# A four-layer graph network in fp32: two more dense layers in seven block products, norm sums moved to ScalarE, adjacency blocks kept by DMA

## The chip, the cores and the metric

The kernel runs on one core of a Trainium2 chip. The metric is the device time of one execution in microseconds (us). Before the change the median of three runs is 2434.67 us (2434.01 to 2434.8). TensorE is called PE here (PEld is its weight load), VectorE DVE, ScalarE ACT, GpSimd POOL, and SyncE, which issues most DMAs, SP.

## The reference

There are B = 32 graphs of N = 512 nodes with D = 256 features, and a dense 512 x 512 adjacency for each. Everything is fp32. Each of four layers ends in `x = layernorm(x + layer(x))`:

```
layer 0: h = (1 + eps) x + adj x;  relu(h W1 + b1) W2 + b2            hidden width 512
layer 1: h = adj (x W^T + b);      where(h > 0, h, alpha h)
layer 2: h = layer_norm(x) gamma + beta
         x + relu((adj h) Wrel + b_rel + h Wroot)
layer 3: h = (eps x + adj x) W1 + b1;  silu(rmsnorm(h) w) W2 + b2     hidden width 1024
```

The terms with eps are put on the diagonal of the adjacency ("loops"), so layer 0 multiplies by adj + (1 + eps) I, layers 1 and 2 by adj, layer 3 by adj + eps I.

## The kernel before

**Plan.** The kernel body describes every operation to a planner (`Plan`, L182). An operation may have several ways (engines) with a cost each (L35 to L68). `order` (L304) plays the list forward, gives each operation an engine, a place in that engine's queue and a buffer, and `best` (L298) keeps the rule from `RULES` (L83) whose plan ends first. The instructions are then issued in that fixed order, so each engine works through its queue strictly in order. A rule says by how much the graphs are set apart (period), how fast need grows within a graph (pace), how far apart the last graphs are (last), and how early side work is wanted (near). Up to FLIGHT = 4 graphs are in flight. Buffers come from 38 rooms of 4 KB per partition, 12 small ones and 8 PSUM banks (L437 to L439); the numbers behind a pool say how many must be left for older graphs. All instructions carry line L252, since one helper issues them, so groups are told apart by tile names.

**Seven products.** `seven` (L552) multiplies two 2 x 2 block matrices with seven block products in place of eight (m1 to m7), at the price of sums of blocks: `left_sums` (L570) and `weight_sums` (L586) for the one factor, `right_sums` (L578) for the other. It is used for the aggregation adj x (`aggregate`, L653), for the first dense layer of layers 0 and 3 (`dense_feat`, L693), and for the second dense layer of layer 3, written out in `layer3` (L895 to L935). The sums of blocks may run on DVE or on POOL.

**Plain dense layers.** The second dense layer of layer 0 (L817 to L819), that of layer 1, and the two of layer 2 (L860 to L865) are done by `dense_tok` (L681): for each half of the nodes, 2 chunks by 4 factors, 16 products with 256 columns per layer and graph in layers 0 and 2, which are added to the residual on DVE by one 512-wide add per half.

**Norms.** `Norm.half` (L755) takes mean and variance of each 128-node chunk by DVE's batch-norm pair (stats and aggregate). `scales` (L761) makes 1/sqrt(var + eps) with a power on POOL, and `scaled` (L769) applies it, per chunk on ACT or DVE.

**Loops.** `Adjacency.sums` (L615) forms the block sums of an adjacency and copies the diagonal blocks aside (on POOL or ACT), `with_loops` (L636) writes them back with the loop added (POOL or DVE), `restore` (L632) writes them back plain (POOL or ACT).

**Queues.** SP's queue holds, in planned order, the loads of adjacencies (4 of 256 KB per graph), of x and of weights, and the stores of the results.

Of the kernel before, what the change touches and what calls it, by code (L numbers as in the profile page):

```python
# [53 lines left out]

def gpsimd_time(n):
    return 0.15 + n * 0.0024, 0.05
# [10 lines left out]
def spread_time():  # L67
# [15 lines left out]
RULES = [  # L83
    (period, pace, 12, near)
    for period, pace in ((60, 1), (76, 1), (84, 2))
    for near in (0, 1, 2, 4)
]
# [94 lines left out]
class Plan:  # L182
# [53 lines left out]
    def do(self, out, *ways, ordered=None):  # L236

        ins = []
        port = set()
        for e, method, _, args, kw in ways:  # L240
            tiles = [x for x in (*args, *kw.values()) if isinstance(x, (bass.AP, Part))]
            ins += tiles
            if e == "gpsimd" and kw.get("op") != ALU.pow or e == "vector" and not (
                method.startswith("bn_") or any(in_psum(x) for x in tiles)
            ):
                port.add(e)

        def issue(engine, method, args, kw):
            def put(x):
                return x.place() if isinstance(x, Part) else x  # L250

            getattr(getattr(self.nc, engine), method)(  # L252
                put(out), *(put(x) for x in args), **{k: put(x) for k, x in kw.items()}
            )

        self.add(
            {
                e: (times, lambda e=e, m=method, args=args, kw=kw: issue(e, m, args, kw))
                for e, method, times, args, kw in ways
            },  # L260
            out, ins, ordered, port,
        )

    def move(self, engine, out, src, times, inward=True):


        def issue():
            getattr(self.nc, engine).dma_start(  # L268
                *(x.place() if isinstance(x, Part) else x for x in (out, src))
            )  # L270

        self.add({engine: (times, issue)}, out if inward else None, [] if inward else [src])
# [114 lines left out]
def tile_gnn_stack(ctx: ExitStack, tc: tile.TileContext, a: dict, out: bass.AP):  # L387
# [36 lines left out]
    FLIGHT, ROOMS, SMALL = 4, 38, 12  # L424
# [12 lines left out]
    banks = pool(psum, "ps", 8, N, N, (0, 2, 2))  # L437
# [23 lines left out]

    def copy(o, x):
        plan.do(o, scalar(AF.Copy, span(o), x), vector("tensor_copy", span(o), x))
# [17 lines left out]
    def stt(o, x, s, y, op0, op1):  # L481
        plan.do(o, vector("scalar_tensor_tensor", span(o), x, s, y, op0=op0, op1=op1))

# [64 lines left out]
    mhalf = constant("mhalf", [P, 2 * NC])  # L548
    nc.vector.memset(mhalf, -0.5)
# [20 lines left out]
    def left_sums(left, a21, s):  # L570

        sub(s[2], left["m1"], a21, vector, gpsimd)
        add(s[0], a21, left["m4"], vector, gpsimd)
        sub(s[1], s[0], left["m1"], vector, gpsimd)
        sub(s[3], left["m2"], s[1], vector, gpsimd)
        left.update(m5=s[0], m6=s[1], m7=s[2], m3=s[3])

    def right_sums(b11, b12, b21, b22, t):  # L578

        sub(t[0], b12, b11)  # L580
        sub(t[1], b22, t[0])
        sub(t[2], b22, b12, vector, gpsimd)
        sub(t[3], b21, t[1], vector, gpsimd)
        return dict(m1=b11, m2=b21, m3=b22, m4=t[3], m5=t[0], m6=t[1], m7=t[2])
# [8 lines left out]
    def quarters(W):  # L593

        n = W.shape[-1] // 2
        return (W[:, k, i * n : (i + 1) * n] for i in range(2) for k in range(2))


    class Adjacency:
# [15 lines left out]
        def sums(self):  # L615
# [6 lines left out]
                with_diagonal.strided(0, (N + P, HC), (TH, 2), (1, P)),  # L622
            ]
            kept = room(4 * HC, P)
            self.plain = [
                kept[:, 0:HC], kept[:, HC : 2 * HC],
                kept[:, 2 * HC :].then(lambda v: v.rearrange("p (k s) n -> p k s n", s=2)),
            ]
            for d, o in zip(self.plain, self.loops):
                plan.do(d, gpsimd("tensor_copy", span(o), o), scalar(AF.Copy, span(o), o))  # L630

        def restore(self):  # L632
            for d, o in zip(self.plain, self.loops):
                plan.do(o, gpsimd("tensor_copy", span(o), d), scalar(AF.Copy, span(o), d))

        def with_loops(self, loop):  # L636
            for d, o in zip(self.plain, self.loops):
                wide = loop.unsqueeze(1)
                if len(o.shape) == 4:
                    wide = wide.unsqueeze(1)  # L640
                add(o, d, wide.to_broadcast(list(o.shape)), gpsimd, vector)

        def row_sums(self):
# [3 lines left out]
            add(rows[:, TH:N], s1[:, 0, :], s1[:, 1, :], gpsimd, vector)  # L647
            add(rows[:, 0:TH], a11[:, 0, :], a11[:, 1, :], gpsimd, vector)
            for k in range(HC):
                add(rows[:, 0:TH], rows[:, 0:TH], a12[:, k, :], gpsimd, vector)  # L650
            return rows

    def aggregate(x, adjacency):  # L653
# [6 lines left out]
        right = right_sums(*blocks, [t[:, i] for i in range(4)])  # L660
# [32 lines left out]
    def dense_feat(aT, left, bias, hT, done):  # L693
# [3 lines left out]
        t = room(4, TH)  # L697
        right = right_sums(
            *(aT[:, k, j * TH : (j + 1) * TH] for k in range(2) for j in range(2)),
            [t[:, i, :] for i in range(4)],  # L700
        )
# [24 lines left out]

    def column_sums(t, put):
# [16 lines left out]
    class Norm:  # L744


        def __init__(self, r):
            self.r = r
            few = small(64)
            cut = lambda at, n: few[:, at : at + n]  # L750
            self.st = [cut(6 * c, 6) for c in range(NC)]
            self.mv = cut(24, 2 * NC).then(lambda v: v.rearrange("p (c i) -> p c i", i=2))
            self.ve, self.rstd, self.shift = (cut(32 + 8 * i, 8) for i in range(3))

        def half(self, h):  # L755
            for c in range(h * HC, (h + 1) * HC):
                r = self.r[:, c, :]
                plan.do(self.st[c], ("vector", "bn_stats", stats_time(D), (r,), {}))
                plan.do(self.mv[:, c, :], ("vector", "bn_aggr", stats_time(6), (self.st[c],), {}))

        def scales(self, *affine):  # L761

            n = self.n = len(affine) * NC
            for i, (m, plus) in enumerate(affine):
                o = self.ve[:, i * NC : (i + 1) * NC]
                ts(o, self.mv[:, :, 1], m, plus, ALU.mult, ALU.add)
            inv_sqrt(self.rstd[:, 0:n], self.ve[:, 0:n])

        def scaled(self, i=0):  # L769
# [3 lines left out]
            stt(shift, self.mv[:, :, 0], -1.0, s, ALU.mult, ALU.mult)  # L773
            for c in range(NC):
# [4 lines left out]
                        "tensor_scalar", D, r, self.mv[:, c, 0:1], scale,  # L779
                        op0=ALU.subtract, op1=ALU.mult,  # L780
# [27 lines left out]
    def layer0(x, adjacency):  # L808
# [8 lines left out]
        for h in range(2):  # L817
            ps = dense_tok([(h1.chunk(k), W2_0[:, k, :]) for k in range(FC0)], h)
            add(half(x, h), ps, half(x, h))  # L819
            norm.half(h)  # L820
# [29 lines left out]
    def layer2(h, xx, u, adjacency):  # L850
# [9 lines left out]
        for h in range(2):  # L860
            ps = dense_tok(
                [(hT.chunk(k), Wroot[:, k, :]) for k in range(DC)]
                + [(aT[:, k, :], Wrel[:, k, :]) for k in range(DC)], h,
            )
            add(half(u, h), ps, half(u, h))  # L865
            stt(half(xx, h), half(u, h), 0.0, half(xx, h), ALU.max, ALU.add)
            norm.half(h)
        adjacency.with_loops(loop3)
# [3 lines left out]
    def layer3(x, adjacency, b):  # L872
# [5 lines left out]
        def squares(f):  # L878
            sq = room(2, N)
            act(sq, hT.pair(f), AF.Square)  # L880
            if f == 0:
                add(acc, sq[:, 0, :], sq[:, 1, :], vector, gpsimd)
            else:
                add(acc, acc, sq[:, 0, :], vector, gpsimd)
                add(acc, acc, sq[:, 1, :], vector, gpsimd)
# [9 lines left out]
        t1, t2, t4 = (room(FH, TH) for _ in range(3))  # L895
        for q in range(0, FH, 2):
# [3 lines left out]
            b11, b12 = (hT.pair(q)[:, :, j * TH : (j + 1) * TH] for j in range(2))  # L900
            b22 = hT.pair(FH + q)[:, :, TH:N]
            t1q, t2q = t1[:, q : q + 2], t2[:, q : q + 2]
            sub(t1q, b12, b11)
            sub(t2q, b22, t1q)
            sub(b12, b22, b12, vector, gpsimd)
            sub(t4[:, q : q + 2], hT.pair(FH + q)[:, :, 0:TH], t2q, vector, gpsimd)
        norm = Norm(x)

        def block(i, j):
            return x[:, j * HC : (j + 1) * HC, i * P : (i + 1) * P]  # L910

        def factor(m, k):
            if m in ("m4", "m5", "m6"):
                return dict(m4=t4, m5=t1, m6=t2)[m][:, k, :]
            f = k if m in ("m1", "m7") else FH + k
            j = 0 if m in ("m1", "m2") else 1
            return hT.chunk(f)[:, j * TH : (j + 1) * TH]

        def product(m, ps, first):
            for k in range(FH):  # L920
                for i in range(HC):
                    mm(
                        ps[:, i, :], factor(m, k)[:, i * P : (i + 1) * P], A2_3[m][:, k, :],
                        first and i == 0 and k == 0, k == FH - 1,
                    )

        def take(ps, i, j):
            add(block(i, j), ps, block(i, j))

        def put(ps, i, j, more):  # L930
            take(ps, i, j)
            if i == 1:
                norm.half(j)

        seven(*(bank(HC, P) for _ in range(3)), product, take, put)  # L935
# [17 lines left out]
    W2_0 = weight("L0_gnn_W2")  # L953
    alpha = row("L1_gnn_alpha")
# [12 lines left out]
    add(shift_2, shift_2, b_2)  # L967
    h = layer1(x, adjacency)
# [9 lines left out]
    A2_3 = weight_sums(  # L978
        "A2_3",
        *(W2_3[:, k * FH : (k + 1) * FH, i * P : (i + 1) * P] for i in range(2) for k in range(2)),  # L980
    )
# [47 lines left out]
```

## Time and profile before

| | |
|---|---|
| profiled execution | 2439.81 us, span of the records 2438.0 us |
| median of the three runs | 2434.67 us |
| granted TensorE clock | 0.997 on average |
| PE, PEld busy | 98%, 87% of the span |
| DVE busy | 2050.2 us, 84% |
| ACT busy | 1226.0 us, 50% |
| POOL busy | 622.6 us, 26% |
| q1, the queue of the DMAs from SP | 71.05 MB, 8.7% of 16 DMA engines |

The busy time of an engine is the union of its instructions' times. Instructions of one engine overlap at their ends, so the mean time of one is longer than the step from one start to the next. An fp32 product appears in the profile as two MATMUL records and two LDWEIGHTS records: 1536 records of one group are 768 products, or 24 per graph.

### The profile page before, as it was taken

Reading aid. Unit: us, or ns where it says so; the run is one execution under the profiler, and the core shown is the slowest. Engines: PE = TensorE matmul, PEld = TensorE weight load, DVE = VectorE, ACT = ScalarE, POOL = GpSimd, SP = SyncE. Lnnn points to the kernel's source line nnn. Section 1 sums busy time; section 2 is a strip of 40 time slices with the busy share of each in tenths; the row PEclk is TensorE's granted clock in tenths of the full one; section 3 lists DMA queues with packets and bytes.
Section 4 is the critical chain, followed back from the end, with each engine's and each line's share of the span. In section 5 each row is a group of like instructions: output and inputs, shape, how many; then the busy total and the mean of one; then the engine's idle time right before and its main releaser. Section 6 shows DMA issues by size and latency. Waiting matters only on the chain.

```text
span 2438.0 us, 35804 instructions
## 1 busy us (share of the span) xinstructions
PE 2387.9 (98%) x12808; PEld 2117.5 (87%) x12808; DVE 2050.2 (84%) x5249; ACT 1226.0 (50%) x2490; POOL 622.6 (26%) x677
## 2 busy tenths in 40 slices
PE   7999999999999999999999999999999999999998
PEld 6888888888888888888888888888888888888888
DVE  7888888788888889888898788988888888888788
ACT  3454545545455454554554544545445455454464
POOL 2232222222222212232122232223222222222220
PEclk9999999999999999999999999999999999999999
DMA  5011001110011110111101111011110011101000
GB/s 177 1 35 35 10 26 35 36 35 10 27 35 35 35 35 1 35 35 35 35 1 35 35 35 36 1 35 35 35 35 9 28 35 36 35 1 35 1 1 35
DMA packets 34915, 73.89 MB, mean 30 GB/s; under 512 B 6832, under 2 KB 9648, under 8 KB 34736
## 3 DMA queue, kind: packets, MB, share of 16 engines
q1 hardware_dynamic: 30576, 71.05, 8.7%
q8 instruction: 101, 1.65, 0.3%
q10 hardware_dynamic: 4160, 0.54, 0.1%
q14 instruction: 78, 0.64, 0.1%
HBM read 54.80 MB, written 16.78 MB: 29 GB/s over the span
## 4 chain that ended last, share of the span: by engine, by line
PE 71%; DVE 23%; ACT 2%; DMA 2%; issue 1%; SPq 0%; POOL 0%; POOLq 0%; ACTq 0%; DVEq 0%
PE ps L252 71%; DVE room L252 19%; DVE few L252 4%; ACT room L252 2%; DMA room<-in_adj_dram 1%; DMA L_gnn_b<-in_L_gnn_b_dram 0%; SPq L268 0%; DMA room<-in_x_dram 0%; POOL few L252 0%; POOL room L252 0%; ACT L252 0%; POOLq L1025 0%; DVEq L252 0%; ACTq L1025 0%; ACTq L252 0%
## 5 line engine op out<-in xcount | busy, mean ns | idle before, releaser
L252 PE MATMUL ps<-room,room 128*128 128x256 f32 x3584 | 872.5, 382 | 20.7 <-DMA room<-in_x_dram 9.9
L252 PEld LDWEIGHTS ps<-room,room 128*128 128x128 f32 x3584 | 672.5, 191 | 122.3 <-DVE room L252 14.5
L252 DVE TENSOR_TENSOR room<-ps,room 128x256 f32<-128x256 f32 (+1 forms) x1024 | 523.7, 522 | 232.8 <-PE ps L252 194.6
L252 PE MATMUL ps<-L_gnn_W,room 128*128 128x128 f32 (+1 forms) x3584 | 623.0, 322 | 5.3 <-ACT room L252 3.4
L252 ACT ACTIVATE room<-room 128x1024 f32<-128x1024 f32 (+2 forms) x421 | 324.3, 773 | 564.2 <-DVE room L252 293.9
L252 PEld LDWEIGHTS ps<-L_gnn_W,room 128*128 128x128 f32 x3584 | 538.4, 191 | 58.1 <-ACT room L252 8.6
L252 DVE TENSOR_TENSOR room<-room,room 128x512 f32<-128x512 f32 (+1 forms) x825 | 491.4, 603 | 17.1 <-DMA room<-in_adj_dram 7.4
L252 POOL TENSOR_TENSOR few<-few,mhalf 128x4 f32<-128x4 f32 (+1 forms) x160 | 191.1, 1195 | 861.1 <-DVE few L252 860.7
L252 PE MATMUL ps<-room,L_gnn_W 128*128 128x256 f32 x1536 | 395.8, 380 | 2.2 <-DVE room L252 2.1
L252 ACT ACTIVATE room<-ps,L_gnn_b_c 128x256 f32<-128x256 f32 x768 | 314.5, 469 | 154.3 <-PE ps L252 149.8
L252 ACT ACTIVATE room<-ps 128x256 f32<-128x256 f32 (+1 forms) x510 | 200.5, 404 | 334.0 <-PE ps L252 327.9
L252 ACT ACTIVATE room<-room,few 128x256 f32<-128x256 f32 x531 | 282.9, 590 | 80.3 <-DVE few L252 79.6
L252 PEld LDWEIGHTS ps<-room,L_gnn_W 128*128 128x128 f32 x1536 | 286.8, 190 | 41.5 <-DVE room L252 4.8
L252 DVE TENSOR_TENSOR room<-room 128x256 f32<-128x256 f32 (+1 forms) x490 | 240.6, 505 | 82.3 <-DMA room<-in_adj_dram 62.3
L252 PE MATMUL ps<-room,A 128*128 128x256 f32 x1152 | 286.1, 380 | 1.1 <-DVE room L252 0.7
L252 POOL TENSOR_TENSOR room<-room,L_gnn_b 128x256 f32<-128x256 f32 x256 | 191.7, 764 | 324.4 <-PE ps L252 164.4
L252 PEld LDWEIGHTS ps<-room,A 128*128 128x128 f32 x1152 | 213.8, 190 | 30.1 <-ACT room L252 1.8
L252 POOL TENSOR_TENSOR room<-room,room 128x512 f32<-128x512 f32 (+1 forms) x103 | 117.0, 1137 | 380.5 <-ACT room L252 165.8
L252 PE MATMUL ps<-A,room 128*128 128x128 f32 x1536 | 195.8, 277 | 11.3 <-DVE room L252 11.1
L252 ACT ACTIVATE room<-room,L_gnn_rms_weight_c 128x512 f32<-128x512 f32 x256 | 168.8, 714 | 68.5 <-DVE room L252 68.1
L252 PEld LDWEIGHTS ps<-A,room 128*128 128x128 f32 x1536 | 184.3, 192 | 21.0 <-DVE room L252 16.3
L252 DVE BATCH_NORM_STATS2 few<-room 128x6 f32<-128x256 f32 x512 | 198.2, 403 | 0.4
(49 smaller groups left out, 1537.4 us busy)
## 6 DMA issues: line engine op xcount, KB each, us to landing
room<-in_adj_dram SPq DMA_DIRECT2D x128, 256.0 KB, 4.8
room<-in_x_dram SPq DMA_DIRECT2D x32, 512.0 KB, 5.8
out_dram<-room SPq DMA_DIRECT2D x32, 512.0 KB, 3.0
L_gnn_W<-in_L_gnn_W_dram SPq DMA_DIRECT2D x2, 1024.0 KB, 8.2
L_gnn_W<-in_L_gnn_W_dram SPq DMA_DIRECT2D x2, 512.0 KB, 6.8
L_gnn_b<-in_L_gnn_b_dram ACTq DMA_DIRECT2D x3, 128.0 KB, 4.2
L_gnn_W_rel<-in_L_gnn_W_rel_dram SPq DMA_DIRECT2D x1, 256.0 KB, 5.6
L_gnn_W_root<-in_L_gnn_W_root_dram SPq DMA_DIRECT2D x1, 256.0 KB, 5.3
```

Source lines behind the costliest of these rows:

```text
L252: getattr(getattr(self.nc, engine), method)(put(out), *(put(x) for x in args), **{k: put(x) for k, x in kw.items()})
```

## The change

1. The second dense layer of layer 0, and both dense layers of layer 2 as one, are done in seven products (`dense_add`, fed by `dense_sums`), as layer 3's was; layer 3 now calls the same two functions. For it the weights `A2_0` and `A_2` are summed once at the start.
2. `Norm.half` no longer uses DVE's batch-norm pair. ACT sums each chunk (`Identity` with an accumulator output), DVE turns the sums of two chunks into minus the mean, ACT sums the squares of x minus mean (`Square` with that bias), and `scales` and `scaled` work from these.
3. The diagonal blocks are kept and put back by DMAs within SBUF, issued from SP: four copies and four restores of 128 KB per graph, in place of three and three operations on POOL or ACT.
4. The sums of blocks, of rows and the loop adds are on DVE alone; POOL keeps the bias rows (`plus_row`) and the powers. `right_sums` puts one of its results in place, so that a room less is needed.
5. The planner gets other rules (period 50, pace 2, last 12 or 20, near 2), 36 rooms in place of 38, and keeps one PSUM bank instead of two for older graphs. The order before was made by period 84, pace 2, last 12, near 2; the one after by period 50, pace 2, last 20, near 2.

```diff
-RULES = [
-    (period, pace, 12, near)
-    for period, pace in ((60, 1), (76, 1), (84, 2))
-    for near in (0, 1, 2, 4)
-]
+RULES = [(50, 2, last, 2) for last in (12, 20)]
...
-    FLIGHT, ROOMS, SMALL = 4, 38, 12
+    FLIGHT, ROOMS, SMALL = 4, 36, 12
...
-    banks = pool(psum, "ps", 8, N, N, (0, 2, 2))
+    banks = pool(psum, "ps", 8, N, N, (0, 1, 1))
...
+    def total(o, x, func, **kw):
+        way = "scalar", "activation", total_time(span(x)), (x,), dict(func=func, **kw)
+        plan.do(o, way, scrap=scrap[:, 0 : span(x)])
...
+    def carry(o, x):
+        plan.move("sync", o, x, move_time(P * span(o) / 256))
...
-        sub(s[2], left["m1"], a21, vector, gpsimd)
+        sub(s[2], left["m1"], a21)
...
             for d, o in zip(self.plain, self.loops):
-                plan.do(d, gpsimd("tensor_copy", span(o), o), scalar(AF.Copy, span(o), o))
+                carry(d, o)
...
+    def dense_sums(upper, lower):
+        right = {}
+        for pairs in zip(upper, lower):
+            blocks = [x[:, :, j * TH : (j + 1) * TH] for x in pairs for j in range(2)]
+            sums = right_sums(*blocks, [room(2, TH) for _ in range(3)], blocks[1])
+            for m, x in sums.items():
+                right.setdefault(m, []).extend(x[:, e, :] for e in range(2))
+        return right
+
+    def dense_add(x, right, left, done):
+        def block(i, j):
+            return x[:, j * HC : (j + 1) * HC, i * P : (i + 1) * P]
+        def product(m, ps, first):
+            n = len(right[m])
+            for k in range(n):
+                for i in range(HC):
+                    mm(
+                        ps[:, i, :], right[m][k][:, i * P : (i + 1) * P], left[m][:, k, :],
+                        first and i == 0 and k == 0, k == n - 1,
+                    )
+        def take(ps, i, j):
+            add(block(i, j), ps, block(i, j))
+        def put(ps, i, j, more):
+            take(ps, i, j)
+            if i == 1:
+                done(j)
+        seven(*(bank(HC, P) for _ in range(3)), product, take, put)
...
         def half(self, h):
-            for c in range(h * HC, (h + 1) * HC):
-                r = self.r[:, c, :]
-                plan.do(self.st[c], ("vector", "bn_stats", stats_time(D), (r,), {}))
-                plan.do(self.mv[:, c, :], ("vector", "bn_aggr", stats_time(6), (self.st[c],), {}))
+            chunks = range(h * HC, (h + 1) * HC)
+            for c in chunks:
+                total(self.sums[:, c : c + 1], self.r[:, c, :], AF.Identity)
+            mine = slice(h * HC, (h + 1) * HC)
+            ts(self.less[:, mine], self.sums[:, mine], -1.0 / D, None, ALU.mult)
+            for c in chunks:
+                total(
+                    self.squares[:, c : c + 1], self.r[:, c, :], AF.Square,
+                    bias=self.less[:, c : c + 1],
+                )
...
-        for h in range(2):
-            ps = dense_tok([(h1.chunk(k), W2_0[:, k, :]) for k in range(FC0)], h)
-            add(half(x, h), ps, half(x, h))
-            norm.half(h)
+        dense_add(x, dense_sums(h1.rooms[:1], h1.rooms[1:]), A2_0, norm.half)
...
-        for h in range(2):
-            ps = dense_tok(
-                [(hT.chunk(k), Wroot[:, k, :]) for k in range(DC)]
-                + [(aT[:, k, :], Wrel[:, k, :]) for k in range(DC)], h,
-            )
-            add(half(u, h), ps, half(u, h))
+        def done(h):
             stt(half(xx, h), half(u, h), 0.0, half(xx, h), ALU.max, ALU.add)
             norm.half(h)
+        dense_add(u, dense_sums(hT.rooms, [aT]), A_2, done)
```

## The prediction

> **What bounds the kernel now.** I read the page's busy times first, then the windows, then the chain of the work that ended last, then the groups by shape and the waits.
>
> ```profile
> PE 2387.9 (98%) x12808; PEld 2117.5 (87%) x12808; DVE 2050.2 (84%) x5249; ACT 1226.0 (50%) x2490; POOL 622.6 (26%) x677
> ...
> 600.00:1200.00 600.00, 592.11 (x3193) 526.12 (x3192) 507.62 (x1297) 303.29 (x620) 154.32 (x170) 1.00 0.09 29
> ...
> PE 71%; DVE 23%; ACT 2%; DMA 2%; issue 1%; SPq 0%; POOL 0%; POOLq 0%; ACTq 0%; DVEq 0%
> ```
>
> PE is busy 592 of 600 us in the middle (second number of the window row), at full clock (1.00). The chain is 71% PE, but 23% DVE: where PE pauses, DVE was late. How full PE is shows in the steps between products, read from runs in the timeline (start, length, engine, shape, count):
>
> ```profile
> 1201.22 4.48 PE L252 MATMUL ps<-room,room 128*128 128x256 f32 x20
> 2408.58 3.51 PE L252 MATMUL ps<-A,room 128*128 128x128 f32 x30
> ```
>
> With one record of 0.379 us, 20 records of 256 columns in 4.48 us step by 4.10/19 = 0.2158 us; with one of 0.275, 30 records of 128 columns step by 3.235/29 = 0.1116 us, and the starts of consecutive records give 0.1117 as the median. A product is two records: 0.4316 and 0.2234 us. The groups give 8840 records of 256 columns, 3584 of 128, and 384 of the transposing kind at 0.109: 1907.7 + 400.3 + 41.9 = 2349.9 us of pure PE work. The span of 2438.0 is therefore 9.9 us to the first product, 2349.9 of work, 8.2 after the last product, and 70 of steps longer than these (by the starts, 11 of them in the first 75 us, 59 later, under 2 us per graph). PE's work sets the time, and it has almost no slack to give elsewhere.
>
> **The change part by part.** *Products.* Instruction lists of both kernels: 512 products of 256 columns go in layer 0's second layer and 512 in layer 2's (16 each per graph), and 896 of 128 columns come in each (28). That is -1024 x 0.4316 = -442.0 and +1792 x 0.2234 = +400.3: **-41.6 us**, 1.30 per graph, all on the path. These rows are the nearest possible: layer 3 already runs this very form.
>
> ```profile
> L252 PE MATMUL ps<-A,room 128*128 128x128 f32 x1536 | 195.8, 277 | 11.3 <-DVE room L252 11.1
> L252 PEld LDWEIGHTS ps<-A,room 128*128 128x128 f32 x1536 | 184.3, 192 | 21.0 <-DVE room L252 16.3
> ```
>
> A rule of the Trainium skill speaks against narrowing products: "Larger matmuls are more efficient than smaller matmuls, when possible" (Perfetto Trace Analysis, section Matmuls), and TensorE: Matmul & The Clock Gate (section "Wait — 56ns, not 53.3ns?") puts a fixed cost of about 2.5 ns on each. The row shows the penalty and that it is larger: 111.7 against 215.8/2 = 107.9 ns is 3.8 ns a record; halving 215.8 - 2.5 and adding 2.5 back would give 109.2. By the page the saving would be 442.0 - 3584 x 0.1092 = 50.6 us; I take the row's 41.6. An eighth of the arithmetic goes, 9.4% of the time.
>
> *DVE.* Steps (not lengths) from runs: 0.60 us for 512 wide, 0.335 for 256, 0.33 for stats, 0.09 for aggregates. By the instruction lists: stats and aggregates -512 each (-215); PSUM adds -128 of 512 and +448 of 256 (+73); sums that POOL did or that the new layers need, +324 of 512 and +121 of 256 (+235); loop adds +164 of 256, -62 of 512 (+18); small ones +26; copies and scalings -66 (-22); weights +4. Together +119 us. Against it stands what POOL took from DVE:
>
> ```profile
> L252 DVE TENSOR_TENSOR room<-room,room 128x512 f32<-128x512 f32 x422 | 318.2, 760 | 11.2 <-DMA room<-in_adj_dram 7.4 <-ACT room L252 1.0
> L252 DVE TENSOR_TENSOR room<-room,ps 128x512 f32<-128x512 f32 x256 | 161.0, 676 | 1.7 <-PE ps L252 1.6
> ```
>
> The same add takes 676 ns with an operand in PSUM and 760 on average with both in SBUF; by single records it takes 680, or about 1230 when a POOL tensor operation runs beside it. Over all DVE groups such overlength is 90 us, 68 of it beside POOL operations that the change takes away. So DVE goes to about 2050 + 119 - 68 = 2101 us, 88% of the new span. It stays below PE, so I cost it at nothing; the cover is the 250 us that DVE still idles, and without it each late DVE microsecond is a PE one.
>
> *ACT.* 1024 accumulating activations of 256 come. No row shows one. Below stands the plain 128x256 activation (414 ns), beside it
>
> ```profile
> L252 ACT ACTIVATE room<-room,few 128x256 f32<-128x256 f32 x531 | 282.9, 590 | 80.3 <-DVE few L252 79.6
> ```
>
> and above it, should the accumulator be read by a step of its own, about twice the first, 0.83. I take 0.59, which has the operand of the new `Square`: +604, less 82 for the diagonal copies that go, plus 32 for work DVE sheds: ACT 1780 us, 74%. At 0.83 it is 2026, 84%, still under PE. The cost is latency: in the old norm the last half needs stats and aggregates (2 x 0.42) before the power; now two sums, a mean, two squares, with four changes of engine: 2 x 1.1 + 0.16 + some 0.4 = 2.8 us, so +2 us per norm. Over most of the run other graphs' products cover it. By the instruction order PE has, from layer 0's last product to layer 1's first, 12 to 24 us of other work before and 8.6 to 11 after; from layer 2 to layer 3, 8 to 11 before and 10 to 11 after. Chain from rows: 0.7 (drain, add), 2.8, scale 0.26, power 1.06, shift 0.26, two scalings 1.1: 6.2 us, plus queueing on busy engines of perhaps 2. It fits, narrowly.
>
> *Loop blocks.* 256 DMAs of 128 KB come onto SP's queue. The nearest rows are the store of 512 KB (3.0 us from issue to landing) and the adjacency load of 256 KB (4.8); an ACT copy took 0.42. DMA: Bandwidth & Descriptors ("Anatomy of one DMA") has 2.0 us plus bytes/436 GB/s, so 2.3; I take 3 to 4.8, the rows. Restores have layer 0's dense layers and norm to land in, 20 us or more: nothing. Queue: in the new order a graph's copies and restores follow its own loads and stand ahead of the next graph's loads, so a load that waits for a room holds none of them up; behind a restore wait only later loads. For the first graph nothing hides the copies: the loop adds wait on them, PE on these. Bounds 0 and 4.4; I take **+3 us**.
>
> *End.* The last norm's extra 2 us has no cover: **+1.5** (part overlaps the last adds).
>
> *New sums.* Layer 3's A products wait for DVE: by the starts of records they carry 20.6 us of long steps after the first 75 us, the largest group. The new layers have half its sums per layer, twice: 0 to 20.6 us. I take **+8**, since the first products need no sum. POOL's clashes: their going may take away none of the 59 us, or 25 (half of PE's waits for DVE and what follows them); I take **-5**.
>
> Sum on the profiled execution: 9.9 + (2349.9 - 41.6) + (11 + 3) + 59 + (8.2 + 1.5) + 8 - 5 = 2403.9 us of span. The median lies 3.3 below the span (2434.67 against 2438.0; the profiled time itself is 2439.81): **2401 us**, -1.4%.
>
> **Rivals.** (a) *Stalls shrink.* DVE is no longer hit by POOL, and new sums find cover: 2401 - 8 - 20 = 2373. For it: 68 us of unplanned DVE length go, and fixed orders suffer from the unplanned. Against it: DVE is fuller. Chance 0.2. (b) *DVE sums pace the new layers* as in layer 3, at the full 20.6, and POOL's going gives nothing: 2401 + 12.6 + 5 = 2419. For it: layer 0's second layer starts 1 us after its first in the new order. Against: two to three other graphs interleave. Chance 0.2. (c) *The norm runs out of cover, slower.* Place: between layer 0 and layer 1, where cover falls from 12-24 to 8.6-11 us. It decides when the chain with its queueing exceeds the cover by 34/32 = 1.05 us per graph; at 2 us, 64 us: 2465. For it: chain 6.2 us without queueing, ACT busier by half. Against: the shortest cover is 2.4 us longer, and before the change layers 2 to 3 lived on 8 to 11 us. Chance 0.06. That the products are not saved is excluded by the instruction lists.
>
> **How the numbers follow.** The sum holds with 0.5, its own range 2390 to 2412; 0.2 for (a), 0.2 for (b), 0.06 for (c), and 0.04 for a loss that ends near no change. Range 2372 to 2428: it takes in the times of (a) and (b), and leaves out (c) and half of what lies around (a). A measurement of this kernel tells 0.2% (5 us) from no change: faster 0.91, same 0.04, slower 0.05.
>
> **What would show it.** Right: about 14,344 PE records, 6792 of 256 and 7168 of 128 columns at the same steps; 2308 us of work; long steps 65 to 80 us; DVE 2080 to 2120 and ACT 1700 to 1850 busy. The two-SBUF add falls from 760 to near 690 ns. Wrong: an accumulating activation beyond 0.8 us, PE waiting for DVE or ACT for over 100 us, or SP copies that land after 6 us with PE behind them.

## The result and the profile after

The changed kernel takes 2399.51 us (median of four runs, 2397.68 to 2405.51) against 2434.74: ratio 0.9857, 95% interval 0.9836 to 0.9878, 1.4% faster. The forecast was 2401. The profiled execution took 2397.68 us, its span 2395.8. The page's busy times, the window row of the middle (PE busy and count, then PEld, DVE, ACT, POOL), and the rows of the groups that were shown before:

```profile
PE 2347.5 (98%) x14344; PEld 2126.5 (89%) x14344; DVE 2128.4 (89%) x5292; ACT 1691.9 (71%) x4438; POOL 387.4 (16%) x422
```

```profile
600.00:1200.00 600.00, 598.69 (x3681) 545.20 (x3680) 542.51 (x1357) 435.99 (x1150) 100.47 (x110) 1.00 0.14 43
```

```profile
L257 DVE TENSOR_TENSOR room<-room,room 128x512 f32<-128x512 f32 x672 | 458.1, 686 | 13.3 <-DMA room<-in_adj_dram 9.9 <-ACT room L257 1.0
L257 PE MATMUL ps<-A,room 128*128 128x128 f32 x3072 | 449.3, 276 | 3.0 <-ACT room L257 1.5 <-DVE room L257 1.1 <-DVE few L257 0.2
L257 ACT ACTIVATE scrap<-room,few 128x256 f32<-128x256 f32 x512 | 258.9, 506 | 43.2 <-DVE few L257 36.5
L257 ACT ACTIVATE scrap<-room 128x256 f32<-128x256 f32 x512 | 212.2, 415 | 69.2 <-DVE room L257 51.8 <-DVE few L257 1.7 <-DMA room<-in_adj_dram 1.5
L257 ACT ACTIVATION_READ_ACCUMULATOR scrap<-room,few 128x1 f32 x512 | 97.2, 190 | 0.0
L257 ACT ACTIVATION_READ_ACCUMULATOR scrap<-room 128x1 f32 x512 | 96.0, 188 | 0.0
```

In the middle PE idles 1.3 us of 600 where it idled 7.9. The two-SBUF add fell from 760 to 686 ns, since POOL works beside it less. DVE is fuller than before (2128 against 2050 us), and each accumulating activation brings a second instruction, the readout. PE's waits for the other two engines (total, times, longest):

```profile
PE ps L257 <- ACT room L257: 13.2, 23, 1.8
PE ps L257 <- DVE room L257: 12.3, 14, 2.8
```

The DMA issues (count, size, us to landing) have the loop copies as

```profile
room<-room SPq DMA_DIRECT2D x256, 128.0 KB, 2.2
```

To see where time went, I take the starts of all product records, and call **long steps** what exceeds the plain step (215.8, 111.7 or 109.3 ns). Span = time to the first product + plain work + long steps + time after the last product. The same sum for every kernel below, with long steps split by stretch (first 75 us, middle, last 300 us):

```
kernel      us       first  work    long: start  middle  end   sum    after last
before      2434.7    9.9   2350.0        11.0    53.8    5.0   69.7    8.4
after       2399.5   10.3   2308.4        16.9    31.1   18.8   66.7   10.4
p_off       2406.3   11.6   2350.0        12.5     3.6   16.6   32.7   10.4
v_off       2469.6   11.3   2308.4        19.2    90.6   28.8  138.6    9.7
r_off       2540.3   10.6   2308.4        19.1   165.6   18.2  203.0   15.7
n_off       2438.9   11.2   2308.4        19.3    66.0   29.7  115.0    8.2
b_r         2432.9   10.9   2350.0         9.1    43.0   12.4   64.5    8.2
b_v         2464.4   10.5   2350.0         7.2    81.2    5.4   93.9    8.4
b_vr        2387.8   10.6   2350.0         4.9     2.7    9.1   16.7    8.2
b_p         2488.2   11.4   2308.4        16.1   130.6   11.8  158.5    8.4
bvr_n       2407.2   11.3   2350.0         6.6    13.0   14.4   34.0   10.5
l_act       2403.8   11.1   2308.4        14.6    24.2   33.2   72.0   10.5
l0_off      2398.9   11.5   2308.4        16.1    32.5   18.7   67.2   10.2
best_2_12   2396.9   11.0   2308.4        17.6    29.8   17.2   64.6    8.0
```

(us: median of all runs; the rest from each profiled execution, whose span can differ from the median by some us; that of `n_off`, 2444.65 us, was the slowest of its 16.) Long steps hold waits and also steps at a lower clock: the trace gives the granted clock as full or half, and by single records the half-clock steps make 1 to 5 us of the sum in most kernels, 7 to 12 in `v_off`, `n_off`, `b_v`, `b_p` and `l_act`, and 22 in `r_off`.

The work fell by the forecast 41.6 us: the counts are the forecast ones (6792 records of 256 columns, 7168 of 128), and the median steps are those of before (216 and 112 ns). The long steps came out near the sum in total (66.7; the sum had 76), but not in place: the middle lost 23 us, start and end gave back 20. Of the signs that the prediction named, counts, work, long steps and the two-SBUF add came out as it said; DVE (2128 us) and ACT (1692) lie 8 us outside their ranges. A right total could still hide wrong terms, and the experiments look for them.

### The profile page after: what moved, and what is told of

It reads as the page before. It is cut to its first block, busy times and chain, and to the rows that moved or that the text cites. A ratio compares the mean times of both kernels' runs of the same rounds, so it can differ in the third digit from the quotient of the medians.

```text
span 2395.8 us, 41267 instructions
## 1 busy us (share of the span) xinstructions
PE 2347.5 (98%) x14344; PEld 2126.5 (89%) x14344; DVE 2128.4 (89%) x5292; ACT 1691.9 (71%) x4438; POOL 387.4 (16%) x422
## 4 chain that ended last, share of the span: by engine, by line
PE 62%; DVE 6%; ACT 4%; DMA 2%; issue 1%; SPq 0%; POOL 0%; POOLq 0%; ACTq 0%; DVEq 0%
PE ps L257 62%; DVE room L257 5%; ACT room L257 2%; ACT scrap L257 2%; DMA room<-in_adj_dram 2%; DVE few L257 1%; DMA room<-room 1%; SPq L271 0%; POOL few L257 0%; POOLq L1038 0%; ACTq L1038 0%; DVEq L257 0%; ACTq L257 0%; POOLq L257 0%
## 5 line engine op out<-in xcount | busy, mean ns | idle before, releaser
L257 PE MATMUL ps<-room,room 128*128 128x256 f32 x3584 | 912.6, 383 | 19.4 <-DMA room<-in_x_dram 11.1
L257 DVE TENSOR_TENSOR room<-ps,room 128x256 f32<-128x256 f32 (+1 forms) x1344 | 608.7, 475 | 114.7 <-PE ps L257 105.0
L257 DVE TENSOR_TENSOR room<-room,room 128x512 f32<-128x512 f32 (+1 forms) x1120 | 635.1, 581 | 25.3 <-ACT room L257 12.7
L257 PE MATMUL ps<-L_gnn_W,room 128*128 128x128 f32 (+1 forms) x3584 | 586.2, 292 | 9.6 <-ACT room L257 6.8
L257 PE MATMUL ps<-A,room 128*128 128x128 f32 x3072 | 449.3, 276 | 3.0 <-ACT room L257 1.5
L257 PEld LDWEIGHTS ps<-A,room 128*128 128x128 f32 x3072 | 405.7, 192 | 15.3 <-DVE room L257 2.4
L257 DVE TENSOR_TENSOR room<-room 128x256 f32<-128x256 f32 (+1 forms) x640 | 318.7, 505 | 47.2 <-DMA room<-in_adj_dram 26.1
L257 ACT ACTIVATE room<-room 128x1024 f32<-128x1024 f32 (+1 forms) x256 | 239.6, 948 | 100.5 <-DVE room L257 99.7
L257 ACT ACTIVATE scrap<-room,few 128x256 f32<-128x256 f32 x512 | 258.9, 506 | 43.2 <-DVE few L257 36.5
L257 ACT ACTIVATE scrap<-room 128x256 f32<-128x256 f32 x512 | 212.2, 415 | 69.2 <-DVE room L257 51.8
```

Of the source, the lines that this page charges most:

```text
L257: getattr(getattr(self.nc, engine), method)(to, *(put(x) for x in args), **kw)
```

## The experiments

**Each part undone in the changed kernel.** In all but `r_off` the planner is held to the rule of the changed kernel (50, 2, 20, 2). Short diffs against the changed kernel:

```diff
# p_off: plain products in layers 0 and 2 (dense_tok), no A2_0 and A_2
-        dense_add(x, dense_sums(h1.rooms[:1], h1.rooms[1:]), A2_0, norm.half)
+        for h in range(2):
+            ps = dense_tok([(h1.chunk(k), W2_0[:, k, :]) for k in range(FC0)], h)
...
# v_off: GpSimd beside VectorE again (block sums, row sums, loop adds, sums of squares)
-        add(s[0], a21, left["m4"])
+        add(s[0], a21, left["m4"], vector, gpsimd)
...
# r_off: the rule of the order before
-RULES = [(50, 2, last, 2) for last in (12, 20)]
+RULES = [(84, 2, 12, 2)]
# n_off: Norm as in the kernel before (bn_stats, bn_aggr)
```

p_off, plain products:

> The changed kernel with the second dense layers of layers 0 and 2 as plain products again (16 of 256 columns each), all else and the planner's rule as in the changed kernel. Theory (TensorE's work sets the time, the narrower products cost 111.7 ns a record): work rises by 41.6 to 2350 us, long steps stay within 10 us of the 66 of the changed kernel, so 2441 us (2431 to 2451). Rival (the narrow products bring long steps of their own, which go with them): work +41.6, long steps -15 or more, 2425 us or less.

Measured 2406.31 us, ratio to the kernel before 0.988 (0.9865 to 0.9895). The theory fails and the rival holds: undoing the products costs 7 us, not 41.6. Work rose by 41.6, and long steps fell by 34, to 3.6 in the middle. Its busy times:

```profile
PE 2365.4 (98%) x12808; PEld 2119.4 (88%) x12808; DVE 1958.6 (81%) x4786; ACT 1647.3 (69%) x4360; POOL 393.0 (16%) x422
```

DVE is 170 us less busy than in the changed kernel, which has the sums and the narrower adds of the seven-product layers besides. PE's records follow the order of the plan, so each can be put to its layer. The 27.5 us of long steps that the products bring to the middle then stand for 4 us before products of the two changed layers; 10 stand before the aggregations, 7 before the first dense layers and 6 before layer 3's second. So the products delay others more than themselves. That DVE's 170 us are the cause is the likely reading, not shown by itself: PE's waits put down to ACT rise as much (6.1 to 13.2 us) as those put down to DVE (8.0 to 12.3).

v_off, GpSimd's shares:

> The changed kernel with GpSimd offered again, beside VectorE, for the block sums, row sums, loop adds and sums of squares; it takes some 295 of them. Theory (the long steps in the middle fell from 54 to 31 us because GpSimd no longer lengthens VectorE's adds): they come back, 45 to 55 us in the middle, 2415 to 2425 us in all. Rival (the new spacing of the graphs did it): middle within 8 us of 31, time within 8 us of 2399.5.

Measured 2469.56 us, ratio 1.0138 (1.0123 to 1.0153): the theory's direction, three times its size. Long steps in the middle go from 31 to 91. PE's waits (total, times, longest) and the busy times:

```profile
PE ps L257 <- ACT room L257: 35.1, 27, 2.8
PE ps L257 <- DVE room L257: 34.6, 64, 3.4
```

```profile
PE 2366.0 (96%) x14344; PEld 2133.9 (86%) x14344; DVE 2120.9 (86%) x5033; ACT 1686.8 (68%) x4399; POOL 700.3 (28%) x720
```

POOL does 298 operations more, DVE 259 fewer, and DVE is as busy as in the changed kernel (2121 against 2128 us): what POOL takes off DVE's list it gives back in length. By single records, 82 us of overlength lie beside the operations that POOL took, and the overlength beside the bias rows rises from 43 to 65.

r_off, the old rule:

> The changed kernel planned by the rule that made the order before (period 84, pace 2, last 12, near 2); instructions otherwise the same. Theory (GpSimd's going cut the long steps in the middle): middle stays near 31 us; the end has long steps near 5 rather than 19, so about 2388 us. Rival (the spacing of a third did it): middle back to 50 or more, 2405 to 2420 us.

Measured 2540.29 us, ratio 1.0424 (1.0401 to 1.0447). With nearly the same instructions the order alone costs 141 us: the rival's direction, but neither side expected the size. PE waits for ACT most:

```profile
PE ps L257 <- ACT room L257: 76.2, 87, 2.6
PE ps L257 <- DMA room<-in_x_dram: 19.2, 6, 10.6
PE ps L257 <- DVE room L257: 16.2, 22, 2.7
```

In PE's queue the graph changes from one product to the next 1292 times here and 3322 times in the changed kernel. Under the old rule long runs of one graph stand together. Of the long steps in the middle, 108 us stand before the aggregations of layers 1 to 3, each of which follows a norm (12 in the changed kernel).

n_off, the batch-norm pair on DVE:

> The changed kernel with the batch-norm pair on VectorE again in place of the sums on ScalarE, rule as in the changed kernel. VectorE's busy time rises from 2128 by about 215 us of steps, less some 60 for the small operations and scalings that go, to near 2280 us, 95% of the span. Theory (VectorE must stay below TensorE by a margin, so the seven products need the norm sums elsewhere): long steps rise to over 120 us, 2440 us or more, the gain of the products gone. Rival (VectorE has slack enough and a norm is 2 us shorter): 2395 to 2410 us.

Measured 2438.88 us, ratio 1.0018 (1.001 to 1.0025): close to the theory, though 115 us of long steps and this time lie just under its bounds. Busy times, and PE's largest wait:

```profile
PE 2362.0 (97%) x14344; PEld 2129.9 (87%) x14344; DVE 2260.8 (93%) x5966; ACT 1244.0 (51%) x2484; POOL 443.2 (18%) x422
...
PE ps L257 <- DVE room L257: 41.0, 43, 4.8
```

**Parts alone in the kernel before.** After this I no longer held that PE's work sets the time, and tried the parts by themselves.

```diff
# b_r: the kernel before, new rule
+RULES = [(50, 2, 20, 2)]
# b_v: sums, loop adds on VectorE alone, diagonal copies on ScalarE alone; rule (84, 2, 12, 2)
-        add(s[0], a21, left["m4"], vector, gpsimd)
+        add(s[0], a21, left["m4"])
...
-                plan.do(d, gpsimd("tensor_copy", span(o), o), scalar(AF.Copy, span(o), o))
+                plan.do(d, scalar(AF.Copy, span(o), o))
# b_vr: b_v with RULES = [(50, 2, 20, 2)]
# b_p: dense_add for layers 0 and 2, 36 rooms, rule (84, 2, 12, 2)
```

> The kernel before, planned by the new rule (period 50, pace 2, last 20, near 2), nothing else changed. Theory now (two things had to go for the long steps to go: GpSimd's clashes, and the load on VectorE's queue; the spacing only suits the changed set of instructions): no gain, long steps 60 or more, 2430 us or more. Rival (the spacing of a third by itself removes the 50 us of long steps in the middle): 2385 to 2400 us.

2432.9 us, ratio 0.9993 (0.9985 to 1.0002). No gain from the rule alone. But more than the spacing changed: under this rule the planner gave POOL 893 operations, where it had 677.

```profile
PE 2385.2 (98%) x12808; PEld 2114.1 (87%) x12808; DVE 2038.7 (84%) x5015; ACT 1230.5 (51%) x2508; POOL 834.8 (34%) x893
```

By single records, DVE's overlength beside the operations that POOL took rises from some 70 to some 120 us.

> The kernel before with block sums, row sums, loop adds and sums of squares on VectorE alone and the diagonal copies on ScalarE alone, so that GpSimd keeps the bias rows and powers; rule as before. Theory (clashes alone made the long steps of the middle): VectorE's busy time rises to near 2150 us, yet the middle falls from 54 to 25 us or less, 2410 us or less. Rival (VectorE's load makes them): they rise, 2445 us or more.

2464.44 us, ratio 1.0122 (1.0107 to 1.0137). Slower: the rival's direction, though DVE is only 35 us busier than before (2085), so DVE's load alone hardly explains it. PE's waits put down to ACT, which has all the diagonal copies here, rise from 5.1 to 31.6 us, those put down to DVE fall from 24.7 to 20.7.

> Both: the kernel before without GpSimd's shares, and planned by the new rule. Theory (GpSimd's shares and the spacing belong together; the norm sums and loop DMAs matter once VectorE is full): close to the changed kernel without its products, middle below 20 us, 2400 to 2412 us. Rival (without the norm sums moved to ScalarE, VectorE at some 2150 us is too full): 2425 us or more.

2387.76 us, ratio 0.9809 (0.9793 to 0.9826). Both together take 47 us off, more than the whole change does and more than the theory expected. The page's first row, its chain, and its middle window:

```profile
PE 2359.1 (99%) x12808; PEld 2116.1 (89%) x12808; DVE 2094.0 (88%) x5407; ACT 1256.0 (53%) x2587; POOL 387.6 (16%) x422
...
PE 95%; DVE 3%; DMA 1%; issue 0%; ACT 0%; SPq 0%; POOLq 0%; POOL 0%; ACTq 0%; DVEq 0%
```

```profile
600.00:1200.00 600.00, 600.00 (x3268) 539.68 (x3267) 531.18 (x1374) 315.50 (x656) 97.65 (x106) 1.00 0.09 29
```

PE has no idle time in the middle, and the chain is 95% PE: this kernel has the 41.6 us of extra work and is still ahead, by having 50 us fewer long steps than the changed kernel. DVE is at 88% here without harm.

> The kernel before with the products alone: second dense layers of layers 0 and 2 in seven products, their sums on VectorE or GpSimd as the other sums, 36 rooms; norm, loops and rule as before. Theory (each of the new sums and adds finds VectorE's queue full, so the 41.6 us of work come back as long steps): long steps 110 us or more, 2435 us or more. Rival (TensorE's work sets the time in any order): long steps 70 to 85, 2395 to 2410 us.

2488.19 us, ratio 1.022 (1.0204 to 1.0235): the theory. Put into the kernel before by itself, under the old rule, the part that was to bring the gain makes it slower. Again the new layers hold few of the long steps: of 131 us in the middle, 12 stand before their products, and 78 before those of layer 3's second layer, where the kernel before has 31. The group with the computed factors, old layers and new:

```profile
L248 PE MATMUL ps<-A,room 128*128 128x128 f32 x3072 | 420.3, 278 | 17.1 <-DVE room L248 16.6 <-DVE few L248 0.2
```

**The rest, and a try at the ends.**

```diff
# bvr_n: b_vr with Norm of the changed kernel, 37 rooms
# l_act: the changed kernel, diagonal copies and restores on ScalarE
-                carry(d, o)
+                act(d, o, AF.Copy)
# l0_off: only the first graph's copies
-                carry(d, o)
+                act(d, o, AF.Copy) if plan.graph == 0 else carry(d, o)
# best_2_12: l0_off, batch-norm pair in the last two graphs, RULES = [(50, 2, 12, 2)]
+        return (PairNorm if plan.graph >= B - 2 else SumNorm)(r)
```

> The kernel before without GpSimd's shares and with the new rule (2388 us), with the norm sums on ScalarE added; 37 rooms. Together with the run without products (2406 us, which has the loop DMAs and the new bank rule besides) it tells who costs the 19 us between the two. Theory (the norm sums cost only their longer chain at the end, the loop DMAs the start): 2388 to 2395 us, long steps in the first 75 us near 5. Rival (the norm sums cost it): 2400 us or more.

2407.22 us, ratio 0.989 (0.9874 to 0.9907): the rival. Without the products the norm sums, with one room less, cost 19 us; long steps rise in the middle by 10, at the end by 5, and the time after the last product by 2.3. With the products they save 39 (`n_off`). Of the 10, 8 stand before layer 1's aggregation, the place that rival (c) of the prediction named.

> The changed kernel with all copies of the diagonal blocks on ScalarE instead of DMA, rule as in the changed kernel. Theory (only the first graph's copies are on the path; later ones are covered either way): the first 75 us lose 5 to 8 of their 17 us of long steps, ScalarE gains 75 us of busy time, 2389 to 2396 us. Rival (ScalarE at 74% comes late for TensorE more often than the DMAs did): 2405 us or more.

2403.77 us, ratio 0.988 (0.9865 to 0.9895), 4 us above the changed kernel, against the theory. The middle gains 7 us, the end loses 14, some 4 of it by the clock: in the last 160 us the granted clock was half for 17 us (3.4 in the changed kernel), and in 6 of these PE stood idle.

> The changed kernel with the copies of the first graph's diagonal blocks on ScalarE, the other graphs' by DMA. Theory (the wait of 3.2 us at 11.7 us and its sequel come from these copies): long steps of the first 75 us fall from 17 to 10 to 13, 2392 to 2397 us. Rival (the start is bound by loads and weight sums anyway): within 3 us of 2399.5.

2398.91 us, ratio 0.9855 (0.984 to 0.9869): no difference. In the changed kernel the wait is plain; the copies leave SP at 10.51 us, land, and DVE and PE go on:

```profile
10.29 2.07 PE L257 MATMUL ps<-room,room 128*128 128x256 f32 x4 [10.29 <-DMA room<-in_x_dram]
10.51 2.77 SPq L271 DMA_DIRECT2D room<-room  x4
...
14.67 0.79 DVE L257 TENSOR_TENSOR room<-room,loop 128x256 f32<-128x256 f32 x2 [2.84 <-DMA room<-room]
...
15.15 0.79 PE L257 MATMUL ps<-room,room 128*128 128x256 f32 x1 [2.79 <-DVE room L257]
```

With the copies on ScalarE this wait is gone, and PE runs 12 records on end; but the first product starts at 11.5 us, and the start's long steps are 16.1 of 16.9. Other waits took its place.

> The same with the batch-norm pair on VectorE for the last two graphs, and last 12: a try at both ends of the run. Theory (the end's 19 us of long steps come from the last graphs' longer norm chain with too little other work beside it): long steps of the last 300 us fall below 12 and the time after the last product from 10.4 to 8.4, 2380 to 2388 us. Rival (the last graph's root-mean-square step and its 56 products stand alone in any case): 2392 us or more.

2396.85 us, ratio 0.9844 (0.9829 to 0.9858): the time after the last product falls to 8.0 as expected, the long steps of the end only from 18.8 to 17.2. The fastest kernel of the study stays `b_vr`.

## Why the prediction was right, and where its steps were not

That the total came within 2 us is luck: the work was sized right, but large terms that the sum had wrong or did not have cancelled.

**The work.** Right to the tenth: -41.6 us by the row of layer 3's records; the estimate from the fixed cost per product that the Trainium skill states (TensorE: Matmul & The Clock Gate, "Wait — 56ns, not 53.3ns?") was 50.6.

**"All on the path".** This step failed. The forecast put the 41.6 us on the path because PE was 98% busy. From `p_off` to the changed kernel, 41.6 us of work go, 34 of long steps come, and the time falls by 7. New sums were put at +8, with 20.6 us as upper end. The upper end was too low, because it priced the waits of the new layers alone: in the middle these are 4 us, while 23 came in other layers. The planner could have told part of this beforehand: the end time that its `order` returns, the start of the last operation, is 2373.4 us for `p_off` and 2358.6 for the changed kernel, so it held the products worth 15 us, not 41.6.

**Item 5, the rule.** The sum had no term for it. It said that the order interleaves two to three graphs, and gave the new order no price. The runs show a gain that neither the rule (-2) nor POOL's leaving (+30) has alone and both have together (-47). The forecast held POOL's leaving worth 5 us, at most 25. So a gain of 47 that had no term met a saving of 41.6 that was worth 7, and norm sums that cost 19 where nothing but their end was priced. In runs, one after the other: before 2434.7, without POOL's shares and with the new rule 2387.8, norm sums added 2407.2, loop DMAs, fewer rooms and the bank rule 2406.3, products 2399.5. The order of this list matters: norm sums first cost, and after the products they save.

**DVE "below PE, at nothing".** Its size was near (2128 us, forecast 2101; the clashes with the bias rows rose from 22 to 43 us). Its price was not nothing: with the norm pair back on it (`n_off`) the time rises by 39 us. The cover was misread too; 250 us of idle DVE is 303 by the prediction's own 2404 and 2101.

**ACT.** 1692 us, forecast 1780. The readout does come as a step of its own, but overlaps its activation: 0.42 + 0.19 us take 0.51 from start to end, 0.51 + 0.19 take 0.60. That is 0.56 on average against the 0.59 taken, some 36 of the 88 us; the rest is not broken down.

**Loop DMAs.** 2.2 us to landing; the rows taken (3 to 4.8) were too far in size and kind. The Trainium skill's 2.0 us plus bytes/436 GB/s (DMA: Bandwidth & Descriptors, "Anatomy of one DMA") gave the better estimate, 2.3, though the page states it for DMAs issued from GpSimd and these come from SP. The start lost 5.9 us against +3, but `l0_off` shows that the copies are not its cause by themselves.

**The end.** After the last product +2.0, forecast +1.5. The long steps of the last 300 us, 5.0 to 18.8, were not forecast. Before the last graph's final products PE waits, and then runs at half clock for a while (the third column from the end is the granted clock; the 0.77 of the second row falls after the last product, which ends at 2385.5 us):

```profile
2360.00:2380.00 20.00, 17.12 (x133) 16.51 (x132) 16.62 (x39) 11.47 (x27) 2.39 (x2) 0.91 0.07 27
2380.00:2396.00 16.00, 5.02 (x43) 4.64 (x41) 4.20 (x16) 7.61 (x24) 2.01 (x2) 0.77 0.16 66
```

**Rivals.** (a) was what happened in the middle (-23 us), offset at the ends; (b) is half right: the products do bring long steps, 34 us of them, but few in the new layers. (c) did not decide: layer 1's aggregation, where cover fell to 8.6 us, carries 6 us of long steps in the middle. Its mechanism shows where the order is another, though: in `r_off`, and in `bvr_n` with 8 us at that very place.

**What stays open.** Why the rule and POOL's leaving help only together is answered in part by the end times that `order` returns for the four kernels, each from its own planner and rule:

```
kernel   plan ends   measured   beyond the plan
before    2385.1      2434.7       49.6
b_r       2375.8      2432.9       57.1
b_v       2440.1      2464.4       24.3
b_vr      2371.7      2387.8       16.1
```

With POOL's shares the execution falls behind its plan by 50 us or more, without them by 24 or less. But under the old rule the plan itself gets 55 us longer without them, and under the new rule 4 shorter; so only both together gain. Why the old rule makes so long a plan of the same work is not shown. PE's queue changes graph 1280 to 1470 times in the kernels with the old rule and 3190 to 4180 times in those with the new one; that waits hide better behind finely mixed graphs fits this: `b_r`, with 3741 changes, has a short plan too, and `r_off`'s plan ends at 2462.0 us, 103 after that of the changed kernel. It is argued, not shown. Nor does DVE's busy share by itself say when waits begin: 88% leaves 2.7 us in the middle of `b_vr`, 85% leaves 81 in `b_v`. Each kernel is also another order out of one planner, so differences of 5 us between them need not be of the part that was changed.

## What to carry to other kernels

A saving on an engine that is 98% busy need not be worth its size: here 41.6 us less work for PE, bought with 170 us more for DVE, was worth 7. Count what the saving adds to the next-fullest engine and expect part of it back, also in places that the change doesn't touch. Where order is planned, a change of the planner's rule is a part of the change like any other: undo it alone before giving the gain to the arithmetic, and see what else the planner moves when the rule changes. Ask the planner for its own end time first. And a right total is no proof of its terms.

## What the runs showed of the hardware

An ACT instruction with an accumulator output is followed by a readout of its own, 188 to 190 ns long. A DMA of 128 KB within SBUF, issued from SP, landed 2.2 us after issue (median of 256). Handing 298 operations to POOL left DVE as busy as it was (2121 against 2128 us), since DVE's own operations beside them became longer. With nearly the same instructions in another order, one core's time rose by 141 us.
